# An attention network in one launch: in its first phase, buffers are taken in another order, more steps run side by side, and some work changes engine

## The chip, the cores and the metric

The program runs on one core of a Trainium2 chip. The metric is the device time of one execution in microseconds (us). A core has a matrix engine (TensorE, in the profile PE, its weight loads PEld), VectorE (DVE), ScalarE (ACT), GpSimd (POOL) and a queue engine (SyncE, SP) that issues transfers here. Each engine works through its own list of instructions in order and waits at semaphores for the others. Before the change the time is 3989.45 us, the median of three runs (3988.71 to 3994.0).

## What is computed

The input is a batch of 32 sequences of 256 tokens with 256 features, float32 throughout. Two layers follow each other. The change is in the first layer, up to its router; this is the kernel's first phase. Cut to what matters, for each sequence:

```python
k  = modulated(x, cond)                       # 256x256 matrix, scaled by the condition
# softmax over the 16 heads of each token: weights q_h . q_h', used on the same 16 heads
o0 = head_softmax_attention(k)
x0 = modulated(o0, cond)
# attention 1 over the 256 tokens, 16 heads of 16, on normed queries and keys
a  = softmax(norm(Q) @ norm(K).T / 4) @ V     # from x0
a  = a * sigmoid(g) * sigmoid(mean(gelu(x0 @ Wg1.T + bg1) @ Wg2.T + bg2))
x1 = x + a @ Wo.T + bo
c2 = x1 + relu(x1 @ w_down) @ w_up            # 256x64 and 64x256, scaled by the condition
h  = layer_norm(c2)
c2 = c2 + attention_2(h)                      # plain queries and keys
logits = layer_norm(c2) @ wr                  # for the router of the second phase
```

The second phase (from the router on: eight experts, the second layer, a butterfly network) uses some of the same helpers. It begins when all 32 sequences are through the first phase.

## The kernel before

**Staging.** One sequence is written as a Python generator, `sequence(b, exact)`. It issues its instructions in steps, and ahead of each it yields the engine and a length, for instance `yield PE, 1.75`. `side_by_side` is a planner: it holds all 32 generators and always lets that step go next which can start first by its own bookkeeping of engines and lengths. So the order of the instructions on each engine is fixed when the program is built; on the chip nothing is reordered. A step that calls another generator with `Part(...)` and yields it runs beside its caller from there on; `yield "join", part` waits for its end.

**Buffers.** `ring` makes a pool of n tiles with a queue of turns (`Turns(n)`), `get` waits for a turn and takes a tile, `back` returns it. `mm` has 3 PSUM tiles, `sh` 12 tiles of 128x512 in SBUF, `hp` 3 large ones, `kk` 2, `qk` 3, `kT` 3, `x1` 3, `c2` 3. `lanes = Turns(6)` lets six sequences be on the way at once.

**One sequence, step by step**, with the lines of the kernel before:

- xT is loaded (L830), scaled on ScalarE (L833), multiplied on TensorE (L252), moved out by ScalarE (L841), transposed back (L246), and copied twice side by side into `kk` by ScalarE (L851).
- `head_softmax_attention` (`exact` is False on the branch that runs): VectorE multiplies `kk` with itself shifted by j heads (L490) and sums over 16 features (L495), for j from 0 to 8; ScalarE takes the exponential (L518); `mirror` on GpSimd fills j from 9 to 15 from these by symmetry with 14 small copies (L503, L504); VectorE sums the weights (L523), inverts (L524), multiplies each weight with its window of `kk` (L531) and adds up in a tree (L539 to L543). The tile `hex` holds the weights as [token half, j, head].
- `transposed` transposes a tile on TensorE (L240) and moves it out on ScalarE (L289, L293). Here and in most steps the PSUM tile is taken from `mm` before the SBUF tile for the result.
- `gate_of_heads` (L764 to L784) runs to its end before attention 1 begins.
- `attention`: `cosine_queries_and_keys` does the two token halves one after the other: projection (L566), bias (L573), squares on ScalarE (L576), sums (L579); then a power on GpSimd (L208, L210) and the scaling (L559), which is a part of its own. Then scores (L716, four 32-row tiles of the array at once), exponentials on ScalarE (L725, 128x2048 at a time), answers (L698, four 32-column tiles at once), copies (L705), transposes back (L743), and a division (L749, L750), one token half after the other.
- `adapter_weights` makes the two small matrices on GpSimd (L795 to L800); they are used at L906 and L915, with ScalarE's ReLU at L910 between them and VectorE's addition at L919 after them.
- `layer_norm`: VectorE takes the statistics (L306, L307), GpSimd the inverse root (`rsqrt`, L208, L210), VectorE scales (`normalize`, L232).

Of the kernel before, what the change touches and what calls it, by code (L numbers as in the profile page):

```python
# [14 lines left out]
F = mybir.dt.float32  # L15
# [7 lines left out]
P = 128  # L23
# [143 lines left out]
def network(ctx: ExitStack, tc: tile.TileContext, a: dict, out: bass.AP):  # L167
# [113 lines left out]
    def transposed(x2, name, scale=None, bias=None, r="sh"):  # L281

        ps = yield from get("mm", "mm", TS)
        yield PE, 0.55
        transpose2(ps, x2)
        xT = yield from get(r, name, TS)
        if scale is None and bias is None:
            yield ACT, 0.6
            nc.scalar.copy(xT, ps)  # L289
        else:  # L290
            yield ACT, 0.95
            for c in range(2):
                nc.scalar.activation(  # L293
                    xT[:, c, :], ps[:, c, :], AF.Identity, bias=bias(c) if bias else 0.0, scale=scale(c) if scale else 1.0
                )
        yield back("mm")
        return xT

    def layer_norm(sm, x2, name):

        yield DVE, 1.2
        st = sm.tile([P, 2, 6], F, name="st")
        mv = sm.tile([P, 2, 2], F, name="mv")
        rstd = sm.tile([P, 2], F, name="rstd")
        for t in range(2):
            nc.vector.bn_stats(st[:, t, :], x2[:, t, :])  # L306
            nc.vector.bn_aggr(mv[:, t, :], st[:, t, :])  # L307
        yield POOL, 1.0
        rsqrt(rstd, mv[:, :, 1], 2, LN_EPS)
        xh = yield from get("sh", name)  # L310
        yield DVE, 0.75
        normalize(xh, x2, mv, rstd)
        return xh
# [118 lines left out]
    wdn = load_w(wA, "wdn", HID)  # L432
    wup = wA.tile([HID, D], F, name="wup")
    nc.sync.dma_start(wup, a["wup"])
    wr = load_w(wA, "wr", NE)
# [27 lines left out]
    ring(pa, "hp", 3, [P, 8, D])  # L463
    ring(pa, "sh", 12, [P, 2, D])
    ring(pa, "kk", 2, [P, 2, 2 * D])
# [15 lines left out]
    def head_softmax_attention(kk, o0, b, exact):  # L481


        e = sm.tile([P, 2, H, H], F, name="hex", tag="hex", bufs=3)
        for j0 in range(0, 9, 4):
            n = min(4, 9 - j0)
            r = "hp" if n == 4 else "sh"
            pr = yield from get(r, "hprod", [P, 2, n, D])
            yield DVE, 0.57 * n
            nc.vector.tensor_tensor(  # L490
                pr, kk[:, :, :D].unsqueeze(2).to_broadcast([P, 2, n, D]), windows(kk, j0, n), ALU.mult
            )
            for t in range(2):
                yield DVE, 0.3 * n
                nc.vector.tensor_reduce(  # L495
                    e[:, t, j0 : j0 + n, :], pr[:, t].rearrange("p j (h d) -> p j h d", d=DH), AX.X, ALU.add
                )
            yield back(r)
# [8 lines left out]
        if exact:  # L507
            yield POOL, 2.8
            mirror()
            mx = sm.tile([P, 2, H], F, name="hmx")  # L510
            yield DVE, 1.7
            nc.vector.tensor_reduce(mx, e.rearrange("p t j h -> p t h j"), AX.X, ALU.max)
            nc.vector.tensor_tensor(e, e, mx.unsqueeze(2).to_broadcast([P, 2, H, H]), ALU.subtract)
            yield ACT, 0.6
            nc.scalar.activation(e, e, AF.Exp, scale=scale)
        else:
            yield ACT, 0.45
            nc.scalar.activation(e[:, :, :9, :], e[:, :, :9, :], AF.Exp, scale=scale)  # L518
            yield POOL, 2.8
            mirror()  # L520
        rs = rhead[:, 2 * b : 2 * b + 2, :]
        yield DVE, 1.5
        nc.vector.tensor_reduce(rs, e.rearrange("p t j h -> p t h j"), AX.X, ALU.add)  # L523
        nc.vector.reciprocal(rs, rs)  # L524
        for t in range(2):
            prs = []
            for j0 in (0, 8):
# [4 lines left out]
                    pr.rearrange("p j (h d) -> p j h d", d=DH),  # L532
                    e[:, t, j0 : j0 + 8, :].unsqueeze(3).to_broadcast([P, 8, H, DH]),
                    windows(kk, j0, 8)[:, t].rearrange("p j (h d) -> p j h d", d=DH),
# [16 lines left out]
    def cosine_queries_and_keys(hT, qT, kT):  # L551
# [8 lines left out]

        halves = []
        for t in range(2):
            ps = yield from get("mm", "mm", [P, 2 * H, DH])
            yield PE, 1.75
            for c in range(2):
# [3 lines left out]
                )  # L569
            qk = yield from get("sh", "qk", [P, 2 * H, DH])  # L570
            sq = yield from get("sh", "sq", [P, 2 * H, DH])
            yield DVE, 0.7
# [7 lines left out]
            yield back("sh")  # L580
            p = Part(normed(qk, n2))
            yield p
            halves.append((p, qk))
        for p, _ in halves:
            yield "join", p
        for side in range(2):
            ps = yield from get("mm", "mm", TS)
# [83 lines left out]

    def attention(l, hT, o_n, b, exact):

# [8 lines left out]
        else:  # L682
            yield from plain_queries_and_keys(hT, qT, kT)
            yield vals
        yield "join", vals
        yield back("sh")
# [51 lines left out]
        yield "back", vaug_turn[l]  # L738
        for t in range(2):
            ps = yield from get("mm", "mm", [P, H, 32])  # L740
# [14 lines left out]
            )  # L755
            yield back("mm")
        yield back("avT")

    def gate_of_heads(x0T, gate, bgate):

        ps = yield from get("mm", "mm", TS)
        yield PE, 0.9
        for c in range(2):
            nc.tensor.matmul(ps[:, 0, :], wg1[:, c, :], x0T[:, c, :], start=(c == 0), stop=(c == 1))  # L764
        gj = yield from get("sh", "gj", [P, S])
        gs = sm.tile([P, 1], F, name="gs")
# [19 lines left out]
    def adapter_weights(b, wd, wu):  # L786
        g1 = yield from get("sh", "dgbb", [P, 2 * HID])
        g2 = yield from get("sh", "ugbb", [HID, 2 * D])
        yield SP, 0.1
        nc.sync.dma_start(g1, gtab[b : b + 1, : 2 * HID].to_broadcast([P, 2 * HID]))  # L790
        yield SP, 0.1
        nc.sync.dma_start(g2, gtab[b : b + 1, 2 * HID :].to_broadcast([HID, 2 * D]))
        yield None, 2.5
# [27 lines left out]

    lanes = Turns(6)

    def sequence(b, exact):
# [7 lines left out]
        for c in range(2):  # L832
            nc.scalar.mul(xT[:, c, :], xT[:, c, :], sty["k"][:, c, b : b + 1])  # L833
        ps = yield from get("mm", "mm", TS)
        yield PE, 1.75
        project_T(ps, wT["k"], xT)
        yield back("sh")
        kxT = yield from get("sh", "kxT", TS)
        yield ACT, 1.05
        for m in range(2):  # L840
            nc.scalar.activation(  # L841
                kxT[:, m, :], ps[:, m, :], AF.Identity, bias=col("kb", m), scale=dem["k"][:, m, b : b + 1]
            )
        yield back("mm")
        ps = yield from get("mm", "mm", [P, 2, D])
        yield PE, 0.55
        transpose2_back(ps, kxT)
        yield back("sh")
        kk = yield from get("kk", "kk")
        yield ACT, 1.05  # L850
# [7 lines left out]
        o0T = yield from transposed(o0, "o0T", scale=lambda c: sty["o"][:, c, b : b + 1])  # L858
        yield back("sh")
        ps = yield from get("mm", "mm", TS)  # L860
        yield PE, 1.75
        project_T(ps, wT["o"], o0T)
        yield back("sh")
        x0T = yield from get("sh", "x0T", TS)
        yield ACT, 1.05
# [8 lines left out]
        bgate = sm.tile([P, 2], F, name="bgate")  # L874
        yield from gate_of_heads(x0T, gate, bgate)
        o_n = yield from get("sh", "o_n")
        yield from attention(1, x0T, o_n, b, exact)
        x = yield from get("sh", "x")
        res = Part(residual_in(b, x))
        yield res  # L880
        wd = sm.tile([P, 2, HID], F, name="wd", bufs=2)
        wu = sm.tile([HID, D], F, name="wu", bufs=2)
        wts = Part(adapter_weights(b, wd, wu))
# [3 lines left out]
        )  # L887
        yield back("sh")
        ps = yield from get("mm", "mm", [P, 2, D])
        yield PE, 1.75  # L890
        project(ps, oT, wout[1])
        yield back("sh")
        yield "join", res
        x1 = yield from get("x1", "x1")
        yield DVE, 0.7
# [3 lines left out]


        x1T = yield from transposed(x1, "x1T")
        yield "join", wts
        ps = yield from get("mm", "mm", TS)
        yield PE, 0.9
        for c in range(2):
            nc.tensor.matmul(ps[:HID, 0, :], wd[:, c, :], x1T[:, c, :], start=(c == 0), stop=(c == 1))  # L906
        yield back("sh")
        act = yield from get("sh", "act", [HID, S])
        yield ACT, 0.5
        nc.scalar.activation(act, ps[:HID, 0, :], AF.Relu)  # L910
        yield back("mm")
        ps = yield from get("mm", "mm", [P, 2, D])
        yield PE, 0.9
        for t in range(2):
            nc.tensor.matmul(ps[:, t, :], act[:, t * P : (t + 1) * P], wu, start=True, stop=True)  # L915
        yield back("sh")
        c2 = yield from get("c2", "c2")
        yield DVE, 0.7
        nc.vector.tensor_add(c2, ps, x1)  # L919
        yield back("mm")  # L920


        xh = yield from layer_norm(sm, c2, "xh")
        hT = yield from transposed(xh, "hT", scale=lambda c: col("ln1g", c), bias=lambda c: col("ln1b", c))
# [18 lines left out]
        yield res  # L943
        xh = yield from layer_norm(sm, c2, "xh")
        yield "join", res
# [1207 lines left out]
```

## Time and profile before

| | us |
|---|---|
| median of three runs | 3989.45 |
| the profiled execution, whole | 3993.62 |
| its span, first to last instruction | 3991.9 |
| first instruction of the head products on VectorE (L490) | 37.67 |
| first scores of an attention on TensorE (L716) | 171.16 |
| last store of the first phase (L948) begins | 1826.43 |
| first instruction of the second phase on VectorE (L1059) | 1834.34 |

Busy in the whole span: PE 3627.3 us, DVE 2471.0 us, ACT 1787.2 us, POOL 1979.5 us.

How to read it: an engine's busy time is the union of its instructions. A group's row gives line, engine, operation, output and input tiles with their shapes and the count, then busy time and mean duration of one instruction, then the idle time of the engine just before these instructions with the one who ended it. Each float32 matmul leaves two records, so counts of PE rows are twice the program's. TensorE's granted clock (PEclk) is a share of full speed.

### The profile page before, as it was taken

How to read it: one execution, taken by the hardware profiler on the slowest of the kernel's cores; microseconds unless marked ns; L12 is line 12 of the kernel's file. 1: busy time of each engine (PE TensorE's matmuls, PEld its weight loads, DVE VectorE, ACT ScalarE, POOL GpSimd, SP SyncE). 2: the span in 40 equal slices, each digit the busy share in tenths (PEclk: the TensorE clock that was granted, in tenths of full speed). 3: DMA queues.
4: the chain of work that ended last, by engine and by line, in shares of the span. 5: the costliest groups of instructions: out<-in, count | busy, mean ns of one | idle time of the engine just before them, and what ended most of it. 6: DMA issues, size and time to landing. Idle time of an engine off the chain costs nothing. (4 is left out here: it accounts for less than half of the span.)

```text
span 3991.9 us, 55591 instructions
## 1 busy us (share of the span) xinstructions
PE 3627.3 (91%) x21868; PEld 2607.7 (65%) x21869; DVE 2471.0 (62%) x3951; ACT 1787.2 (45%) x2682; POOL 1979.5 (50%) x1959
## 2 busy tenths in 40 slices
PE   2689898899999999887999999999898999999999
PEld 2356556566666666552566666666686888888888
DVE  6886898898999999625766452000236464565654
ACT  1367666667777777662222222222222333333333
POOL 4554445545555555420644656554215455565653
PEclk7699999999999999995899999999998999999999
DMA  1001000000000000002233433322242323232331
GB/s 63 5 16 32 22 24 15 26 26 26 26 26 26 27 28 26 23 18 90 74 99 91 106 88 85 62 47 48 67 157 77 104 83 104 88 116 87 100 102 43
DMA packets 134368, 237.17 MB, mean 59 GB/s; under 512 B 19249, under 2 KB 80817, under 8 KB 131538
## 3 DMA queue, kind: packets, MB, share of 16 engines
q0 software_dynamic: 48128, 100.77, 10.4%
q1 hardware_dynamic: 85826, 132.25, 9.9%
q8 instruction: 174, 2.85, 0.3%
q14 instruction: 96, 0.79, 0.1%
q10 hardware_dynamic: 144, 0.52, 0.0%
HBM read 182.99 MB, written 50.48 MB: 58 GB/s over the span
## 5 line engine op out<-in xcount | busy, mean ns | idle before, releaser
L725 ACT ACTIVATE pt<-sc 128x2048 f32<-128x2048 f32 x256 | 480.7, 1878 | 204.1 <-PE sc L716 202.0
L1373 PE MATMUL by<-w,hid 128*128 128x256 f32 x2048 | 452.7, 379 | 2.5 <-DVE ysb L1379 2.5
L1358 PE MATMUL bh<-ehT,w 128*128 128x512 f32 x1024 | 452.3, 595 | 1.5 <-ACT ehT L1327 1.5
L1347 ACT ACTIVATE hid<-bh,cols 128x512 f32<-128x512 f32 x256 | 174.8, 688 | 593.1 <-PE bh L1358 548.2
L1373 PEld LDWEIGHTS by<-w,hid 128*128 128x128 f32 x2048 | 386.5, 190 | 66.3 <-issue 13.9
L210 POOL TENSOR_TENSOR n<-n,negh 128x32 f32<-128x32 f32 x64 | 374.1, 5846 | 5.3
L1281 POOL DMA_INDIRECT rrows<-ysb,row x128 | 223.3, 1745 | 260.5 <-DMA rrows<-ysb,row 139.6
L698 PE MATMUL av<-pt,vaug 128*32 128x256 f32 x4096 | 292.0, 405 | 58.7 <-ACT pt L725 56.5
L1358 PEld LDWEIGHTS bh<-ehT,w 128*128 128x128 f32 x1024 | 194.9, 191 | 222.1 <-issue 215.9
L1379 DVE TENSOR_TENSOR ysb<-by,b 128x512 f32<-128x512 f32 x64 | 44.0, 688 | 454.4 <-PE by L1373 333.3
L716 PE MATMUL sc<-qT,kT 32*128 32x256 f32 x4096 | 306.1, 414 | 19.9 <-ACT pt L725 18.7
L539 DVE TENSOR_TENSOR hprod<-hprod 128x1024 f32<-128x1024 f32 (+2 forms) x384 | 317.0, 825 | 7.1
L531 DVE TENSOR_TENSOR hprod<-hex,kk 128x2048 f32<-128x2048 f32 x128 | 298.5, 2332 | 0.0
L716 PEld LDWEIGHTS sc<-qT,kT 32*128 32x128 f32 x4096 | 192.4, 192 | 131.4 <-issue 66.2
L1314 POOL DMA_INDIRECT xg<-h2buf,tok x128 | 150.3, 1174 | 211.5 <-DVE tok L1173 90.3
L1983 PE MATMUL dh<-zT,w_eff 128*128 128x256 f32 x1024 | 238.8, 383 | 5.7 <-DVE zT L1960 5.7
L698 PEld LDWEIGHTS av<-pt,vaug 128*32 128x32 f32 x4096 | 110.6, 113 | 188.1 <-ACT pt L725 86.3
L1997 PE MATMUL do<-w_con,gT 128*128 128x256 f32 x1024 | 231.7, 380 | 0.0
L1983 PEld LDWEIGHTS dh<-zT,w_eff 128*128 128x128 f32 x1024 | 191.2, 192 | 30.7 <-DVE zT L1960 6.9
L1997 PEld LDWEIGHTS do<-w_con,gT 128*128 128x128 f32 x1024 | 193.4, 191 | 25.4
L503 POOL COPY hex<-hex 128x30 f32<-128x30 f32 (+6 forms) x224 | 53.2, 237 | 308.8 <-ACT hex L518 308.8
L208 POOL TENSOR_SCALAR rstd<-mv 128x2 f32<-128x2 f32 x160 | 44.0, 275 | 317.8 <-DVE mv L307 309.9
(612 smaller groups left out, 7585.6 us busy)
## 6 DMA issues: line engine op xcount, KB each, us to landing
w<-in_w SPq DMA_DIRECT2D x16, 1024.0 KB
x<-rrows SPq DMA_DIRECT2D x64, 256.0 KB
bfw<-in_upw SPq DMA_DIRECT2D x10, 1024.0 KB
bfw<-in_dnw SPq DMA_DIRECT2D x10, 1024.0 KB
xT<-in_xT SPq DMA_DIRECT2D x32, 256.0 KB
x<-in_x SPq DMA_DIRECT2D x32, 256.0 KB
h2buf<-xh SPq DMA_DIRECT2D x32, 256.0 KB
ytbuf<-yT SPq DMA_DIRECT2D x32, 256.0 KB
```

What stands on the lines that cost most here:

```text
L210: nc.gpsimd.tensor_tensor(o, o, negh[:p].to_broadcast([p, n]), ALU.pow)
L531: nc.vector.tensor_tensor(pr.rearrange("p j (h d) -> p j h d", d=DH), e[:, t, j0 : j0 + 8, :].unsqueeze(3).to_broadcast([P, 8, H, DH]), wi ...
L539: nc.vector.tensor_tensor(pr[:, :n], pr[:, :n], pr[:, n : 2 * n], ALU.add)
L698: nc.tensor.matmul(av[32 * i : 32 * i + 32, c % 2, :], va[:, kc, 4 * c + i, :], pt[:, i, kc, :], start=(kc == 0), stop=(kc == 1),)
L716: nc.tensor.matmul(sc[:, i, kc, :], kT[r, m, kc * P : (kc + 1) * P], qT[r, e, m, :], start=True, stop=nm is None,)
L725: nc.scalar.activation(pt, sc, AF.Exp, scale=1.0 / math.sqrt(DH))
L1281: nc.gpsimd.indirect_dma_start(rrows[:, :], bass.IndirectOffsetOnAxis(ap=row[:, j0 + t : j0 + t + 1], axis=0), y[:, t, :], None, compute_o ...
L1347: nc.scalar.activation(o, ps, AF.Relu, bias=bcol)
L1358: nc.tensor.matmul(ps, w["w1"][:, c, f * P : (f + 1) * P], hT[c], start=(c == 0), stop=(c == 1))
L1373: nc.tensor.matmul(ps[:, t, :], hid[f // 4][:, f % 4, (t0 + t) * P : (t0 + t + 1) * P], w["w2"][:, f, :], start=(f == 0), stop=(f == 7),)
L1983: nc.tensor.matmul(ps[:, g, :], w_eff[:, c, f * P : (f + 1) * P], zT[:, c, :], start=(c == 0), stop=(c == 1))
L1997: nc.tensor.matmul(ps[:, t, :], gT[:, f, t * P : (t + 1) * P], w_con[:, f, :], start=(f == 0), stop=(f == 7))
```

## The change

Five things change in the first phase.

1. **Order of taking tiles.** In `transposed`, `half`, `gate_of_heads` and `sequence` the SBUF tile for the result is taken before the PSUM tile. `sh` grows from 12 to 16 tiles, `lanes` from 6 to 7.
2. **More parts.** The two halves of the cosine queries and keys, the two halves of the division after attention, and `gate_of_heads` become parts that run beside each other.
3. **Weights along a diagonal.** `mirror` goes from the branch that runs. `hex` is laid out as 24 rows of 9: rows 8 to 23 hold the heads with their j from 0 to 8, and ScalarE copies rows 16 to 23 to rows 0 to 7. Weights of j from 9 to 15 are read along a diagonal (step 9 between heads, step 8 between j). The sum of the weights takes two reductions and an addition.
4. **Layer norms of the first phase** are scaled on ScalarE with scale and bias per token; GpSimd makes the bias with two more small operations. In the second phase `layer_norm` stays as it was.
5. **Adapter.** Both small products use the array in two 64-wide tiles, one for each token half. `wup` is loaded to both partition halves, and `wu` and `act` fill 128 partitions.

The diff, cut to its core:

```diff
     def transposed(x2, name, scale=None, bias=None, r="sh"):
+        xT = yield from get(r, name, TS)
         ps = yield from get("mm", "mm", TS)
         yield PE, 0.55
         transpose2(ps, x2)
-        xT = yield from get(r, name, TS)
...
-    def layer_norm(sm, x2, name):
+    def layer_norm(sm, x2, name, engine=DVE):
...
         rsqrt(rstd, mv[:, :, 1], 2, LN_EPS)
+        if engine == ACT:
+            less = sm.tile([P, 2], F, name="less")
+            nc.gpsimd.tensor_scalar(less, mv[:, :, 0], -1.0, None, ALU.mult)
+            nc.gpsimd.tensor_tensor(less, less, rstd, ALU.mult)
+            xh = yield from get("sh", name)
+            yield ACT, 0.95
+            for t in range(2):
+                nc.scalar.activation(
+                    xh[:, t, :], x2[:, t, :], AF.Identity, bias=less[:, t : t + 1], scale=rstd[:, t : t + 1]
+                )
+            return xh
...
-    ring(pa, "sh", 12, [P, 2, D])
+    ring(pa, "sh", 16, [P, 2, D])
...
-        e = sm.tile([P, 2, H, H], F, name="hex", tag="hex", bufs=3)
+        hex_ = sm.tile([P, 2, H * H], F, name="hex", tag="hex", bufs=3)
...
+            e = hex_[:, :, : 24 * 9].rearrange("p t (h j) -> p t h j", j=9)
+        def weights(t, j0, n, t1=None):
...
+            if j0 < 8:
+                return e[:, ts, 8:, j0 : j0 + n].rearrange("p t h j -> p t j h")
+            v = e[:, ts, 0:1, 0:1]
+            return bass.AP(v.tensor, v.offset + 9 * 0 + 8 + 8 * (j0 - 8), [v.ap[0], v.ap[1], (8, n), (9, H)])
...
-            nc.scalar.activation(e[:, :, :9, :], e[:, :, :9, :], AF.Exp, scale=scale)
-            yield POOL, 2.8
-            mirror()
+            nc.scalar.activation(e[:, :, 8:, :], e[:, :, 8:, :], AF.Exp, scale=scale)
+            nc.scalar.copy(e[:, :, :8, :], e[:, :, 16:, :])
...
-        nc.vector.tensor_reduce(rs, e.rearrange("p t j h -> p t h j"), AX.X, ALU.add)
+            nc.vector.tensor_reduce(rs, e[:, :, 8:, :], AX.X, ALU.add)
+            nc.vector.tensor_reduce(rs2, weights(0, 9, 7, 2).rearrange("p t j h -> p t h j"), AX.X, ALU.add)
+            nc.vector.tensor_add(rs, rs, rs2)
...
-                    e[:, t, j0 : j0 + 8, :].unsqueeze(3).to_broadcast([P, 8, H, DH]),
+                    weights(t, j0, 8)[:, 0].unsqueeze(3).to_broadcast([P, 8, H, DH]),
...
-        halves = []
-        for t in range(2):
+        def half(t, o):
+            qk = yield from get("sh", "qk", [P, 2 * H, DH])
+            sq = yield from get("sh", "sq", [P, 2 * H, DH])
             ps = yield from get("mm", "mm", [P, 2 * H, DH])
...
+        halves = []
+        for t in range(2):
+            o = []
+            p = Part(half(t, o))
             yield p
...
-        for t in range(2):
+        def tokens(t):
             ps = yield from get("mm", "mm", [P, H, 32])
...
-    lanes = Turns(6)
+    lanes = Turns(7)
+    pair_turn = Turns(1)
...
+        kk = yield from get("kk", "kk")
         ps = yield from get("mm", "mm", [P, 2, D])
         yield PE, 0.55
         transpose2_back(ps, kxT)
         yield back("sh")
-        kk = yield from get("kk", "kk")
...
-        yield from gate_of_heads(x0T, gate, bgate)
+        gates = Part(gate_of_heads(x0T, gate, bgate))
+        yield gates
         o_n = yield from get("sh", "o_n")
-        yield from attention(1, x0T, o_n, b, exact)
+        yield from attention(1, x0T, o_n, b, exact, gates)
...
         for c in range(2):
-            nc.tensor.matmul(ps[:HID, 0, :], wd[:, c, :], x1T[:, c, :], start=(c == 0), stop=(c == 1))
...
+            for t in range(2):
+                nc.tensor.matmul(
+                    ps[t * HID : (t + 1) * HID, 0, :P], wd[:, c, :], x1T[:, c, t * P : (t + 1) * P],
+                    start=(c == 0), stop=(c == 1),
+                )
...
+        c2 = yield from get("c2", "c2")
+        yield pair_turn
+        ps = []
         for t in range(2):
-            nc.tensor.matmul(ps[:, t, :], act[:, t * P : (t + 1) * P], wu, start=True, stop=True)
...
+            ps.append((yield from get("mm", "mm", [P, D])))
+        yield "back", pair_turn
+        yield PE, 0.6
+        for t in range(2):
+            r = slice(t * HID, (t + 1) * HID)
+            nc.tensor.matmul(ps[t], act[r, :], wu[r, :], start=True, stop=True)
...
+        for t in range(2):
+            nc.vector.tensor_add(c2[:, t, :], ps[t], x1[:, t, :])
...
-        xh = yield from layer_norm(sm, c2, "xh")
+        xh = yield from layer_norm(sm, c2, "xh", ACT)
```

The last edit stands twice. The names in the second phase that call the changed `transposed` are `side_part` and `whole`; the second phase's instructions stand in the same order on every engine before and after the change. In the first phase the program before has 7319 instructions on TensorE's list, 2105 on VectorE's, 1618 on ScalarE's and 958 on GpSimd's; the changed one has 7383, 2073, 1778 and 638.

## The prediction, made before the changed kernel ran

> **What bounds the kernel now.** The second phase has the same order of instructions on every engine before and after, so only the first phase counts: 1834.34 us of the span of 3991.9 us. I read the page's slices first, then busy times by stage, then who waited for whom, then the start in order of time, then the groups that the edits touch.
>
> The slices (each 99.8 us):
>
> ```profile
> PE   2689898899999999887999999999898999999999
> DVE  6886898898999999625766452000236464565654
> PEclk7699999999999999995899999999998999999999
> ```
>
> TensorE and VectorE are both nearly full from the third slice to the 17th; TensorE comes late at the start, VectorE ends early.
>
> Busy time by stage (us, instructions in brackets; then granted clock):
>
> ```profile
> 37.00:200.00 163.00, 69.17 (x301) 39.96 (x299) 146.15 (x164) 41.98 (x64) 69.26 (x85) 0.62 0.01 3
> 200.00:830.00 630.00, 561.26 (x4668) 369.24 (x4668) 521.04 (x737) 419.51 (x590) 302.82 (x339) 0.95 0.07 23
> 830.00:1697.00 867.00, 805.89 (x6971) 535.77 (x6969) 760.88 (x1115) 620.59 (x877) 478.85 (x488) 0.99 0.09 26
> 1697.00:1834.00 137.00, 109.38 (x950) 71.08 (x950) 30.08 (x76) 70.56 (x91) 27.59 (x32) 0.85 0.06 20
> ...
> sum 600.00, PE 564.63 PEld 376.57 DVE 543.80 ACT 439.51 POOL 338.16; mean PE 188.21 PEld 125.52 DVE 181.27 ACT 146.50 POOL 112.72
> ```
>
> The columns are PE, PEld, DVE, ACT, POOL. PE is busy 89.1% from 200 to 830 us, 93.0% from 830 to 1697, 79.8% in the tail. The last row covers 1000 to 1600 us by stretches of 200 us. There the loads of xT (L830) start at 1040.82 and, eleven sequences later, at 1585.13: 49.48 us a sequence. Times 188.21/200 that is 46.6 us of PE for each sequence; DVE has 44.8, ACT 36.2, POOL 27.9. So PE is the fullest, VectorE only 1.7 us behind, and some 2.9 us of a sequence's period is PE standing idle.
>
> Who waited, from 37 to 1834 us (total, times, longest):
>
> ```profile
> PE av L698 <- ACT pt L725: 56.5, 41, 2.6
> PE mm L246 <- ACT kk L851: 33.5, 1, 33.5
> PE mm L240 <- ACT kk L851: 31.1, 1, 31.1
> DVE rd L749 <- PE mm L743: 61.8, 13, 20.8
> DVE qk L559 <- POOL n L210: 57.0, 28, 5.3
> DVE rhead L523 <- POOL hex L504: 18.5, 14, 5.1
> ```
>
> The two single waits of over 30 us are the start:
>
> ```profile
> 78.76 0.43 DVE L543 TENSOR_TENSOR o<-o,rhead 128x256 f32<-128x256 f32 x1
> 108.17 1.01 ACT L851 COPY kk<-mm 128x1024 f32<-128x1024 f32 x1 [27.12 <-DVE hprod L531]
> 109.23 1.12 PE L240 MATMUL mm<-ident,o 128*128 128x128 f32 x4 [31.14 <-ACT kk L851]
> ```
>
> The first sequence's o0 is ready at 79.2 us, but its transposition runs at 109.23: ahead of it in PE's list stand transpositions of later sequences, which hold PSUM tiles while they wait for one of two `kk` tiles.
>
> The groups that the edits touch:
>
> ```profile
> L915 PE MATMUL mm<-wu,act 64*128 64x256 f32 x128 | 36.1, 402 | 0.0
> L906 PE MATMUL mm<-x1T,wd 128*64 128x256 f32 x128 | 34.5, 392 | 0.0
> L232 DVE TENSOR_SCALAR xh<-c,mv,rstd 128x256 f32<-128x256 f32 x128 | 48.0, 417 | 20.6 <-POOL rstd L210 20.6
> L523 DVE TENSOR_REDUCE rhead<-hex 128x32 f32<-128x512 f32 x32 | 32.8, 1026 | 18.5 <-POOL hex L504 18.5
> L531 DVE TENSOR_TENSOR hprod<-hex,kk 128x2048 f32<-128x2048 f32 x128 | 298.5, 2332 | 0.0
> ```
>
> **The change, part by part.** Costs are for all 32 sequences.
>
> Adapter: 34.5 + 36.1 = 70.6 us of PE. Two tiles of the array at once halve this: -35 us. That tiles run at once shows in L716, four 32-row tiles: 4096 records of 414 ns mean fill only 306.1 us, and L698 does the same with columns. The other bound: tiles one after the other, L915 unchanged and L906 as 256 records of 128 columns at the 0.16 us (81.6/512) that L743's records take, 41 us instead of 34.5: +6. I take -35, since L716 and L698 are the same kind. These instructions lie on the fullest engine; at 93% busy they are worth 35/0.93 = 38 us. Beside it: `wu` grows to 128 partitions with the same 256 columns, so L799 and L800 keep their times; `ugbb` is twice as many bytes and `wup` one more load on SP's queue, at a DMA share of 0.09 and with nobody waiting for these tiles: nothing. VectorE's addition becomes two of 256 columns, 0.42 us each by L750, for one of 0.68: 5 us of VectorE, beside PE. The pair holds two of three PSUM tiles, which may delay a neighbour; the tiles freed early elsewhere weigh against that, and I take nothing.
>
> Norms: VectorE loses 48.0 us. ScalarE gains 128 instructions of about 0.50 us (L833, the same shape from SBUF): 64 us, 2.0 a sequence, to 38 of 49: it stays below PE. GpSimd gains two small operations per norm, each between 0.36 us (L208 on rstd) and 0.97 (L210 on rstd); I take 0.36, as neither is a power: 46 us, and 0.7 us more before the scaling may start. Behind the waiting scaling on ScalarE stand exponentials (L725), for which PE's answers wait. Bounds: nothing, or all 64 norms late on PE by 0.7, 46 us. Before, PE waited for xh in 9 of 64 norms; nine times 0.7 is 6 us, which I take.
>
> Mirror: GpSimd loses 53.2 us (L503) and 43.6 (L504), VectorE the wait of 18.5 at L523; ScalarE gains a copy of 144 elements, at most L518's 0.44 us, 14 us in all, beside PE's work.
>
> Sum of the weights: L523 reads with a step of 16 words, 1026 ns for 512 elements; L579 reads 512 in a row in 677. New: 288 in a row (0.38), 224 with a step of 8 (0.45 at L523's rate), an addition (0.2): 1.03. Nothing changes; bounds -3 and +10 us. The writes of L495 with a step of 9 are 64 for 1024 reads: nothing.
>
> Diagonal read in L531: bounds are nothing and L523's excess, 0.68 ns, on each of 2048 elements: 1.4 us for each of 128, 179 us of VectorE. I take nothing: each weight is repeated over 16 features, and L531 and L559 read such repeats now without a penalty (2.28 us for 2048, 0.66 at best for 512), so a hop comes once in 16: 11 us at most. VectorE ends at 44.8 - 1.5 + 0.2 = 43.5 us a sequence, under PE's 46.6 - 1.1 = 45.5.
>
> [...]
>
> Order of tiles, parts, lanes: in the changed PE list the first o0 is transposed before the third sequence's kk, and the first scores come before the second sequence's projections; before, two sequences go in lockstep and the first scores run at 171.16. Worth between 0 and 45 us (30 of waiting, 15 of lockstep) of work started earlier; I take 25. It counts only while PE stays the bound to the end, as the sums say. Lanes and `sh` cost no instruction; a tile held longer costs nothing while 16 suffice.
>
> Packing: from 200 to 830 us PE is 89.1% busy; less the adapter's share, 561 - 12 = 549 us take 616 at that and 590 at the 93.0% of the next stage: -26. For it: I counted, by mean durations, the PE work that stands in PE's list between a product and the first matmul that reads its moved-out copy. Under 2.2 us (L725's 1.88 and a hand-over) stand in 304 of 1410 places before and 235 after. Against it: among scores to answers, the dearest wait, it is 58 of 256 before and 62 after. Past 93% I take nothing; at 95% the later stage would give 18 us more.
>
> **Sum**: -38 - 25 - 26 + 6 = -83 us. The profiled execution took 3993.62 us, 4 above the median, so 3910.6 there and 3907 as a median (3989.45 - 83).
>
> **The rivals.** Only the removed work is felt: in-order lists stall as before and no start is gained, -38 + 6 = -32, 3957. For it: the waits of L698, unchanged. Better than forecast: 45 at the start and 95%, -83 - 20 - 18 = -121, 3868. For it: fewer waits through GpSimd. No net effect: the norms' 46 us on ScalarE eat the 38 of the adapter and the order gives nothing: 3997. Slower: the diagonal costs its upper bound in L531. VectorE then needs 43.5 + 4 x 1.4 = 49.1 us a sequence and is the bound; at 94% busy, the best that PE has now, a period of 52.2, 2.7 more than 49.48; over 28 sequences +76, less 25 of the start: +51, 4040. VectorE overtakes PE when L531 passes 2.28 + 0.50 = 2.8 us; the gain is gone near 3.3 us. Against it: L559.
>
> **How the numbers follow.** Forecast 0.56 (own range 3880 to 3940), only work 0.19, better 0.11, no net effect 0.05, slower 0.09. A measurement of this kernel tells about 0.2%, 8 us, from no change. The first three are faster: 0.86; same 0.05; slower 0.09. The range 3855 to 3985 leaves out slower, most of no net effect, and about a third of better.
>
> **What would show it.** Right: the first phase ends near 1750 us, the adapter's two groups near 35 us together, L531's successor at 2.3 us, the waits of 30 us on kk gone, first scores near 125 us, PE at 93% or more from 200 us on, the second phase as long as before. Wrong: L531 at 3 us or more, ScalarE waiting long for GpSimd at the norms with PE behind it, or a tail above 137 us.

## The result, and the profile after

The changed kernel is slower: 4030.22 us, median of four runs (4024.9 to 4034.74), beside 3989.08 for the kernel before on the same chip; the ratio is 1.010, 95% interval 1.0082 to 1.0118. The profiled execution took 4034.14 us, with a span of 4032.4. The second phase begins at 1876.05 us instead of 1834.34; from there to the end of the span it is 2156.4 us, before 2157.6. All of the loss lies in the first phase.

The slices of the page after (PE, DVE, granted clock; each 100.8 us):

```profile
PE   3788999989888988886999999999898999999999
DVE  6889868797888777624766453000136564555654
PEclk7799999899999999997799999999998999999999
```

TensorE starts earlier (3 and 7 instead of 2 and 6), but from the 11th slice to the 18th it stands at 8 but for one, and VectorE is no longer full either. No engine has become the bound: from 830 to 1697 us each of them is busy for less of the time than before. The stages say it in numbers (PE, PEld, DVE, ACT, POOL, then clock):

```profile
37.00:200.00 163.00, 91.24 (x616) 57.72 (x618) 148.44 (x178) 67.65 (x99) 60.01 (x26) 0.74 0.03 8
200.00:830.00 630.00, 558.44 (x4660) 370.14 (x4660) 526.65 (x766) 437.44 (x647) 322.70 (x229) 0.94 0.08 25
830.00:1697.00 867.00, 761.16 (x6430) 506.83 (x6431) 699.67 (x1024) 606.57 (x887) 417.13 (x310) 0.94 0.08 26
```

The 22 us that TensorE gains up to 200 us are there. From 830 to 1697 us it is busy 87.8%, before 93.0%, and its clock is 0.94 instead of 0.99. The start itself, in the trace after:

```profile
79.15 0.90 PE L240 MATMUL mm<-ident,o 128*128 128x128 f32 x3 [14.32 <-DVE o L581]
109.91 2.09 PE L762 MATMUL sc<-qT,kT 32*128 32x256 f32 x16 [0.98 <-ACT kT L646]
```

The transposition of the first o0 runs 30 us earlier and the first scores 61 us earlier. So the start came earlier, as forecast, and was lost again later. Waits of the first phase (total, times, longest):

```profile
ACT xh L317 <- POOL less L313: 83.3, 35, 6.3
PE av L744 <- ACT pt L771: 72.3, 61, 3.9
DVE rhead L559 <- ACT hex L550: 45.2, 18, 5.6
```

The first row is new: at 35 of the 64 norms ScalarE stands, up to 6.3 us, for the product `less` that GpSimd now computes. The answers' wait for exponentials, 56.5 us before, is 72.3. The groups that the edits made:

```profile
L317 ACT ACTIVATE xh<-c,less,rstd 128x256 f32<-128x256 f32 x128 | 69.7, 593 | 83.4 <-POOL less L313 83.3
L979 PE MATMUL mm<-wu,act 64*128 64x256 f32 x128 | 28.1, 469 | 6.4 <-DVE c L1003 6.2 <-DVE qk L611 0.2
L962 PE MATMUL mm<-x1T,wd 128*64 128x128 f32 x256 | 22.4, 299 | 5.3 <-POOL wd L848 3.3 <-ACT x1T L289 2.0
L569 DVE TENSOR_TENSOR hprod<-hex,kk 128x2048 f32<-128x2048 f32 x128 | 297.7, 2325 | 0.0
```

The adapter takes 50.5 us of TensorE instead of 70.6; the diagonal read costs nothing (2325 ns, before 2332).

One norm in order of time shows what a wait of ScalarE does (start, length, engine, line; in brackets the idle time before it):

```profile
1133.54 1.26 POOL L864 TENSOR_TENSOR rs__9374<-x,c 128x512 f32<-128x512 f32 x1
1134.88 0.52 POOL L208 TENSOR_SCALAR rstd<-mv 128x2 f32<-128x2 f32 x1
1135.49 0.77 POOL L210 TENSOR_TENSOR rstd<-rstd,negh 128x2 f32<-128x2 f32 x1
1136.32 0.38 POOL L312 TENSOR_SCALAR less<-mv 128x2 f32<-128x2 f32 x1
1136.52 2.28 DVE L521 TENSOR_TENSOR hprod<-kk 128x2048 f32<-128x2048 f32 x1
1136.79 2.07 POOL L313 TENSOR_TENSOR less<-less,rstd 128x2 f32<-128x2 f32 x1
1138.90 1.09 ACT L317 ACTIVATE xh<-c,less,rstd 128x256 f32<-128x256 f32 x2 [4.79 <-POOL less L313]
1140.05 0.57 ACT L751 COPY avT<-av 128x512 f32<-128x512 f32 x1
1140.67 1.07 PE L744 MATMUL av<-pt,vaug 128*32 128x256 f32 x16 [2.38 <-ACT avT L751]
1141.67 1.89 ACT L771 ACTIVATE pt<-sc 128x2048 f32<-128x2048 f32 x1
```

GpSimd needs 4.0 us from the first of the norm's four operations to the end of the last. In the planner's bookkeeping the whole step has 1.0 (`yield POOL, 1.0` stands ahead of four operations where there were two). ScalarE has come to the norm's place in its list and stands 4.79 us. The copy L751 behind it belongs to another sequence; TensorE's answers wait 2.38 us for that copy, not for the norm. And the exponential L771, whose scores were there at 1138.3, starts 3.4 us later.

### The profile page after: what moved, and what is told of

Its sections match the earlier page's. It is cut to its first block, busy times and chain, and to the rows that moved or that the text cites. A ratio compares the mean times of both kernels' runs of the same rounds, so it can differ in the third digit from the quotient of the medians.

```text
span 4032.4 us, 55509 instructions
## 1 busy us (share of the span) xinstructions
PE 3637.3 (90%) x21997; PEld 2621.0 (65%) x21997; DVE 2424.4 (60%) x3919; ACT 1853.6 (46%) x2842; POOL 1942.9 (48%) x1639
## 5 line engine op out<-in xcount | busy, mean ns | idle before, releaser
L771 ACT ACTIVATE pt<-sc 128x2048 f32<-128x2048 f32 x256 | 481.1, 1879 | 167.6 <-PE sc L762 166.3
L744 PE MATMUL av<-pt,vaug 128*32 128x256 f32 x4096 | 296.4, 410 | 79.2 <-ACT pt L771 72.3
L577 DVE TENSOR_TENSOR hprod<-hprod 128x1024 f32<-128x1024 f32 (+2 forms) x384 | 314.8, 820 | 8.4
L569 DVE TENSOR_TENSOR hprod<-hex,kk 128x2048 f32<-128x2048 f32 x128 | 297.7, 2325 | 0.0
L208 POOL TENSOR_SCALAR n<-n 128x32 f32<-128x32 f32 x64 | 58.7, 917 | 484.0 <-DVE n L617 395.9
L208 POOL TENSOR_SCALAR rstd<-mv 128x2 f32<-128x2 f32 x160 | 52.6, 328 | 383.1 <-DVE mv L307 375.1
```

Source lines behind the costliest of these rows:

```text
L569: nc.vector.tensor_tensor(pr.rearrange("p j (h d) -> p j h d", d=DH), weights(t, j0, 8)[:, 0].unsqueeze(3).to_broadcast([P, 8, H, DH]), wi ...
L577: nc.vector.tensor_tensor(pr[:, :n], pr[:, :n], pr[:, n : 2 * n], ALU.add)
L744: nc.tensor.matmul(av[32 * i : 32 * i + 32, c % 2, :], va[:, kc, 4 * c + i, :], pt[:, i, kc, :], start=(kc == 0), stop=(kc == 1),)
L771: nc.scalar.activation(pt, sc, AF.Exp, scale=1.0 / math.sqrt(DH))
```

## The experiments

Theory L: the order was laid on a length for the norms' GpSimd step that is far too short. Theory N, its strict form: the way through GpSimd costs wherever it is put. Theory D: the exponential and copy of the heads' weights on ScalarE are the loss. Theory S: any new order lands somewhere else, and no edit is to blame. The table has the changed kernel and the 18 runs after it; "length" is what the planner counts for the norms' step on GpSimd, "hand-over" its time between engines, the wait is that of ScalarE for `less` in the first phase. The 1.7, 2.4 and 3.4 in the three rows below the changed kernel, and the 0.25 of "before, replanned", hold for the second phase too; in all other rows the number differs in the first phase alone. The ends and waits are those of one profiled execution each.

| kernel | norms, length | hand-over | median us | ratio to before, 95% | first phase ends | wait |
|---|---|---|---|---|---|---|
| changed | ScalarE, 1.0 | 0.2 | 4030.2 | 1.0082–1.0118 | 1876.1 | 83.3 |
| same, 1.7 | ScalarE, 1.7 | 0.2 | 4023.3 | 1.0061–1.0095 | 1853.8 | 67.6 |
| same, 2.4 | ScalarE, 2.4 | 0.2 | 3970.3 | 0.9936–0.9969 | 1808.2 | 47.8 |
| same, 3.4 | ScalarE, 3.4 | 0.2 | 3970.4 | 0.9928–0.9962 | 1804.9 | 27.3 |
| norms on VectorE | VectorE | 0.2 | 3957.5 | 0.9899–0.9935 | 1797.5 | – |
| changed, replanned | ScalarE, 1.0 | 0.25 | 4012.8 | 1.0042–1.0075 | 1857.0 | 110.2 |
| same, 2.4 | ScalarE, 2.4 | 0.25 | 3965.0 | 0.9926–0.9959 | 1812.7 | 40.5 |
| norms on VectorE | VectorE | 0.25 | 3924.9 | 0.9819–0.9852 | 1768.8 | – |
| before, norms alone | ScalarE, 1.0 | 0.2 | 4074.9 | 1.0187–1.0221 | 1923.4 | 97.0 |
| before, replanned | VectorE | 0.25 | 4014.9 | 1.0037–1.0082 | 1872.6 | – |
| before, replanned | VectorE | 0.15 | 4065.4 | 1.0169–1.0203 | 1911.5 | – |
| before, diagonal alone | VectorE | 0.2 | 4000.2 | 1.0019–1.0040 | 1841.2 | – |
| before, adapter alone | VectorE | 0.2 | 3982.2 | 0.9980–1.0000 | 1826.6 | – |
| order alone | VectorE | 0.2 | 3983.7 | 0.9989–1.0008 | 1828.4 | – |
| changed, mirror on GpSimd | ScalarE, 1.0 | 0.2 | 4054.2 | 1.0135–1.0169 | 1887.7 | 136.5 |
| changed, six lanes | ScalarE, 1.0 | 0.2 | 4046.5 | 1.0118–1.0152 | 1892.5 | 112.7 |
| norms on VectorE, all lengths | VectorE | 0.2 | 3941.5 | 0.9873–0.9906 | 1792.8 | – |
| changed, all lengths | ScalarE, 2.4 | 0.2 | 3957.7 | 0.9920–0.9954 | 1801.6 | 62.5 |
| norms on VectorE, all lengths | VectorE | 0.25 | 3972.1 | 0.9956–0.9977 | 1819.5 | – |

**Norms back on VectorE.**

```diff
-        xh = yield from layer_norm(sm, c2, "xh", ACT)     # both norms
+        xh = yield from layer_norm(sm, c2, "xh")
```

> The changed kernel with one part undone: both norms are scaled by VectorE again, as before the change; all else stays. Theory N (the norms are the loss: ScalarE stands 83 us behind GpSimd's product L313, and the exponentials behind it make TensorE late): about 40 us or more come back, 3990 us or less, and TensorE is above 92% busy between 1000 and 1600 us again. Theory D (the loss is VectorE waiting in order for ScalarE's exponential and copy of the heads' weights): the time stays near 4030 us, since ScalarE loses only 70 us of work. Theory S (each new plan of the order lands somewhere within about 1%, whatever the edit): any time between 3960 and 4060, and nothing to read from it alone.

Measured 3957.5: 73 us come back, nearly twice what the change loses. From 1000 to 1600 us TensorE is busy 91.2%, in the changed kernel 87.4%. D in its plain form falls, since ScalarE's part in the heads' weights is still there.

**Only the number in the planner.**

```diff
-        yield POOL, 1.0
+        yield POOL, 2.4        # then 1.7 and 3.4
         rsqrt(rstd, mv[:, :, 1], 2, LN_EPS)
```

> The changed kernel, in which the planner of the order counts 2.4 us for the norms' four operations on GpSimd instead of 1.0; the trace shows 0.50 + 0.97 + 0.54 + 0.43 us for them. No instruction is changed, only their order. Theory L (the loss comes from the order, which puts ScalarE's scaling where GpSimd cannot have it ready): the waits of 83 us for the product fall below 40, and 20 to 40 us come back, 3990 to 4010. Theory N in its strict form (the way through GpSimd is too long wherever it is placed): 4020 to 4040. Theory S: between 3960 and 4060, with no link between the waits and the time.

> The changed kernel with 1.7 us in the planner for the norms' four operations on GpSimd, between the 1.0 that gave 4030 and the 2.4 that gave 3970. Theory L: between them, 3985 to 4015, and the wait of ScalarE for the product between 48 and 83 us. Theory S: anywhere between 3950 and 4050.

> The same with 3.4 us, one more than the mean of the trace, since single operations there took up to 2.3 us. Theory L: the wait falls further, below 40 us, and the time stays within 10 us of 3970 or goes toward the 3957 of norms on VectorE: 3955 to 3980. Theory S: anywhere between 3950 and 4050.

No instruction differs, and 60 of the 73 us come back at 2.4; L had expected 20 to 40 and a wait below 40 us. Waits in the trace at 2.4:

```profile
ACT xh L317 <- POOL less L313: 47.8, 25, 7.3
PE av L744 <- ACT pt L771: 71.8, 54, 3.5
```

From 1.0 to 3.4 the wait goes 83, 68, 48, 27 us, and the first phase ends at 1876, 1854, 1808, 1805. The whole time at 1.7 is 4023, above L's 3985 to 4015: `layer_norm` serves the second phase too, whose part of the span was 2170 us there and 2166 at 3.4, 2157 at 2.4.

TensorE's wait for the exponentials does not move with the number (72.3 us at 1.0, 71.8 at 2.4; with the norms on VectorE it is 71.6), so the time does not come back there. Among its waits that fall from 1.0 to 2.4 are those for `xh`, from 23.5 to 7.1 us, and for `x1`, the sum before the adapter (L950), from 42 to 14. The number also tells the planner when GpSimd is free again, so it moves other steps than the norms. Through which waits the 60 us come back is not separated.

**The norms alone, on the kernel before.** The edit is `layer_norm` of the change, and nothing else.

> The kernel before with one part of the change alone: both norms scaled by ScalarE, GpSimd's step still counted as 1.0 by the planner of the order. Theory N/L (this part is the loss, because the order expects the product 1.4 us too early): slower than before, by the 30 to 70 us that undoing it gave back, 4020 to 4060, with ScalarE waiting 60 to 120 us for the product. My forecast's own view (6 us): 3995 or less. Theory S (any new order lands within about 1%): 3950 to 4030, no link with that wait.

Measured 4074.9, 83 more and above the 4060 of N and L, with a wait of 97 us. The forecast's 6 us fall.

**Is it luck of an order?** One number of the planner, in the kernel before.

```diff
-LAG = 0.2
+LAG = 0.25      # and, for the first phase alone, 0.15
```

> The kernel before, in which only one number of the planner differs: the hand-over between engines is counted as 0.25 us instead of 0.2. Not one instruction changes, only their order. This measures how far a new order alone moves the time. Theory S: 20 to 40 us either way. Theory L: within 10 us of 3989, since no length in the plan has become wrong.

> The kernel before with the hand-over counted as 0.15 us instead of 0.2 in the planner of the first phase alone; no instruction changes. The other direction of a new order (0.25 ended the first phase 38 us later). Theory S, symmetric: anywhere within 40 us of 3989. If the order of before stands better than its neighbours: later again, 4000 to 4030. Theory L: within 10 us of 3989.

Measured 23 and 76 us slower; L's 10 us were missed both times. S has a point: in the second run a new order alone costs nearly as much as the whole change was to win. With 0.25 the second phase was planned anew too and is 21 us shorter; by the first phase alone the two orders end 38 and 77 us later. Both neighbours are worse, so the order of before stands better than these two. A single comparison of two plans settles nothing below some 80 us, and the norms had to be tried again under a second plan.

**The same pair under a second plan.** The hand-over is 0.25 in the first phase alone, in all three.

> The changed kernel with the hand-over counted as 0.25 us in the planner of the first phase alone; the norms' step stays at 1.0. If the loss comes from the norms' length (N, L) and not from an unlucky order: still slower than before, 4000 to 4060, with 60 us or more of ScalarE waiting for the product. If it was an unlucky order (S): likely below 3990.

> The changed kernel with the norms on VectorE and the hand-over counted as 0.25 us in the first phase alone. N and L: still faster than before, 3935 to 3980, so that the distance to the replanned changed kernel of the same call is 40 to 110 us again. S: the distance shrinks below 30 us or changes its sign.

> The changed kernel with its norms on ScalarE, the hand-over counted as 0.25 us in the first phase, and the norms' four operations on GpSimd counted as 2.4 us instead of 1.0. Under the first plan that one number gave 60 us. Theory L (the order was laid on a length that is too short): 3940 to 3975, 40 to 70 less than the 4012.8 of the same plan at 1.0, and the wait of ScalarE for the product falls from 110 us below 70. Theory N, strict (the way through GpSimd costs wherever it is put, and the first pair was luck): within 20 us of 4013. Theory S: anywhere between 3930 and 4040.

Norms on ScalarE and VectorE: 4012.8 and 3924.9, 88 apart; the second is faster than the 3935 expected at best. With the length at 2.4: 3965.0, 46 less by the ratios. The loss of the norms is thus there under two plans and in the kernel before (73, 88, 83), and the number alone gives 60 and 46 of it. Most of these differences are below 80 us; what speaks for L is that they agree. Whatever else differs in them, the six kernels with the norms on ScalarE and a length of 1.0 or 1.7 take 4012.8 to 4074.9, the four with 2.4 or 3.4 take 3957.7 to 3970.4. ScalarE's wait does not give the time by itself: it is 110.2 us at 4012.8 and 83.3 at 4030.2, 62.5 at 3957.7 and 47.8 at 3970.3. What remains to the norms on VectorE is 13 and some 42 us; how much of that is N and how much another order is open. Fewer GpSimd operations for the product were not tried.

Whether the five parts together lose is another question, and its answer depends on the plan. With 0.25 on both sides the changed kernel's first phase ends 16 us before that of the kernel before (1857.0, 1872.6), with 0.2 it ends 42 us after it.

**The other parts.** The mirror on GpSimd again, in the changed kernel; six lanes; and three parts by themselves: the diagonal read on the kernel before, the adapter on the kernel before, and the order (tiles, parts side by side, seven lanes, 16 tiles) without the other three.

```diff
-    lanes = Turns(7)
+    lanes = Turns(6)
```

> The changed kernel with one part undone: the heads' weights are mirrored by GpSimd again (L503 and L504 of the kernel before) and read in order, one sum over 16. Theory D: VectorE's wait of 45 us for ScalarE at rhead turns back into one of about 18 for GpSimd, the period falls from 56 toward 50 us, about 4000 us. Theory N: GpSimd gets 97 us more work, so its product for the norms comes later still: 4030 to 4070. Theory S: between 3960 and 4060.

> The changed kernel with six sequences in flight instead of seven (the 16 tiles stay). Theory lanes (the seventh sequence adds tiles held and work that stands ahead of older sequences): about 3990. Theories N and D: no more than 10 us either way, 4020 to 4040, since the start is the same and only 49.5 us a sequence is lost later. Theory S: between 3960 and 4060, although not one instruction of the work is changed.

> The kernel before with the diagonal read of the heads' weights alone (no mirror on GpSimd, exponential and copy on ScalarE, two sums on VectorE). The forecast took nothing for this part, 3989. Undoing it in the changed kernel made that 24 us slower, so theory G (GpSimd's 97 us of mirroring stood before the power step and the norms, whose results VectorE and ScalarE wait for) expects 3955 to 3975 and the waits of VectorE at L559 for the power step (57 us before) cut by a third or more. Theory S: within 25 us of 3989 either way, no link with those waits.

> The changed kernel without the adapter's two tiles, without the diagonal read and with the norms on VectorE: what is left is the order of tiles, the parts side by side, seven lanes and 16 tiles. The forecast gave this part 25 us at the start and 26 in the packing: 3938 by it. If only the start is gained (the first scores come 60 us earlier in the trace of the changed kernel, and TensorE does 20 us more by 200 us): 3964 to 3970. If the gain is given back later, TensorE at 89% from 200 to 830 us as before: 3985 or more. A new order alone moved the kernel before by 23 us, so less than that is not told apart.

> The kernel before with the adapter's two tiles of the array alone (and its three PSUM tiles of which the pair takes two). The forecast halved 70.6 us of TensorE and divided by 0.93: 38 less, 3951. By the durations in the trace of the changed kernel (L962 22.4 and L979 28.1 us, 50.5 together) it is 20.1/0.93 = 22 less, 3967. If the pair's PSUM tiles hold up their neighbours: 3980 or more. A new order alone moved the kernel before by 23 us.

The mirror costs 24 us in the changed kernel, 12 of them in the first phase, and its removal 11 us in the kernel before: the sign changes with the plan, so nothing can be said on G's time, and the 24 us may be the order as well. G's sign did come: without the mirror VectorE's wait at the scaling of q and k for the power step falls from 57.0 to 34.7 us. The 4000 us that D expected with the mirror back did not come. Six lanes are slower by 16, so nothing speaks for the seventh as the loss. The adapter alone gives 0.1%; the order alone nothing. Where the start goes is in the stages of the order alone:

```profile
37.00:200.00 163.00, 86.32 (x567) 53.82 (x565) 148.16 (x168) 63.59 (x91) 71.94 (x81) 0.72 0.02 6
830.00:1697.00 867.00, 790.39 (x6657) 527.18 (x6655) 743.97 (x1061) 596.65 (x835) 437.13 (x458) 0.96 0.08 25
```

TensorE does 17 us more by 200 us, and 15.5 us less from 830 to 1697 (790.4, before 805.9).

**All lengths as measured.** Projections 1.95 for 1.75, the power step 6.6 for 5.8, scaling of q and k 1.0 for 0.7, the router 1.1 for 0.4, and so on.

> The changed kernel with the norms on VectorE, and every length in the planner of the first phase set near the mean that the trace of the changed kernel shows (projections 1.95 for 1.75, power step 6.6 for 5.8, router 1.1 for 0.4, adapter 0.7 and 0.9 for 0.6 and 0.6, and so on). Theory L in its wide form (the loss is a plan with wrong lengths, whichever they are): better than the 3957 of norms on VectorE, 3920 to 3950. In its narrow form (only lengths on a chain that makes an engine wait in order matter, and the norms' was the one): within 25 us of 3957. Theory S: 3930 to 4000.

> The changed kernel with its norms on ScalarE, with all lengths of the first phase set as measured, the norms' step on GpSimd at 2.4 us among them. Theory L, wide: below the 3970 of the norms' length alone, 3910 to 3950, since VectorE is 48 us freer than with the norms on it. Narrow: 3945 to 3995. Theory S: 3930 to 4010.

> The changed kernel with the norms on VectorE, all lengths of the first phase as measured and the hand-over at 0.25 us: both steps that were faster, 3941.5 and 3924.9, together. If measured lengths are worth something by themselves: 3900 to 3920. Theory S: between 3915 and 3965, with nothing added up.

3941.5 and 3957.7, by the ratios 11 and 6 us below the kernels without them, but some 50 us worse under the second plan (3972.1, there 3924.9 without them): nothing adds up, and L in its wide form is not borne out. Of the lengths tried, only that of the norms moved the time the same way under both plans. The fastest version is the changed kernel with norms on VectorE and a hand-over of 0.25: 3924.9, ratio 0.9835, 95% interval 0.9819 to 0.9852.

## Why the prediction was wrong, step by step

**Norms: the step that failed.** "Before, PE waited for xh in 9 of 64 norms; nine times 0.7 is 6 us, which I take." It measured +73 to +88. What it counted came near, before and then after:

```profile
PE mm L240 <- DVE xh L232: 14.5, 9, 3.8
PE mm L240 <- ACT xh L317: 23.5, 18, 4.5
```

That is 9 us more; the rest is what the step left out. Three things are wrong in it. It counted only who waits for xh; in the norm shown above, what stands behind the scaling on ScalarE pays too, another sequence's copy and an exponential. The text named such work, and then took nothing for it; what it costs over all 64 norms is not measured. It took 0.36 us for each new GpSimd operation; they take 0.54 and 0.43, and the whole step 2.36 (0.50 + 0.90 + 0.54 + 0.43) after 1.33 before. And it took the order of the changed list as laid out for these lengths: the new step stood under the old `yield POOL, 1.0`. By the runs this is the largest of the three, since that number alone gives 60 and 46 us back. The upper bound of 46 us left it out too, since it counted each norm once on PE.

**Adapter.** The prediction halved 70.6 us of PE and divided by 0.93: 38. In the adapter alone the two groups fall to 47.0 us (24.2 + 22.8), 50.5 in the changed kernel; so the halving is two thirds true. TensorE's busy time in the first phase falls by 20.3 us (1545.7 to 1525.4), its idle time rises by 12.6, and 7.7 us of the first phase are left. The division by 0.93 assumed that idle time shrinks with the work; it grew. How much of that is the adapter and how much the new order is open.

**Start and packing.** The events came (o0 at 79 us, scores at 110), the worth did not. "It counts only while PE stays the bound to the end, as the sums say" is the mistake: sums of busy time say who has most work, not that this engine never waits in its list. Packing took the 93.0% of the regular stage as a property of the work. It changes with the order: 90.2% in the kernel before at a hand-over of 0.25 (781.7 of 867 us), 91.2% in the order alone, 87.8% after.

**The base of the sum.** −83 was counted from an order that is 23 and 76 us better than its replanned neighbours. With the norms on VectorE the rest of the change gave −33 and −64 under two plans, both counted from the order of before, where the terms without the norms summed to −89. At the same hand-over on both sides, the first phase of these kernels ends 37 and 104 us before that of the kernel before (1797.5 and 1834.3, 1768.8 and 1872.6). How much of that each small term gave can't be told apart from what a new plan does.

**What was right.** L531's successor at 2.3 us, TensorE's waits of over 30 us for `kk` gone, the second phase as long as before, the rhead sum (0.45 + 0.55 + 0.20 = 1.20 us) near its 1.03. GpSimd's two operations on `wu` with 128 partitions for 64 take 0.72 us each at the shortest, as before, and 1.06 and 1.05 on the mean, before 0.87 and 1.66. Of the rivals, "no net effect" had the part that loses, the norms' way through GpSimd, at about half its size and without the planner's length; "slower" had the time, 4040, by luck, with a mechanism that L569 refutes (2325 ns, before 2332). The sign named for being wrong, ScalarE waiting long for GpSimd at the norms, is what the trace shows, with PE waiting directly behind it 18 times.

## What to carry to other kernels

In a schedule that is written down when the program is built, a length that is too short on the way to an in-order engine can cost the instructions queued there, not just the one that waits (in the norm shown, 2.38 us for another sequence's answers; the number alone gave 60 and 46 us back under two plans): after moving a step to another engine, correct its length from the trace first. Before giving a cause to one or two per cent, plan the same kernel anew with a neutral number: here that alone moved it by 0.6 and 1.9%, so each cause needs a second plan. Removed work on a 93% busy engine is not time won until its idle time is seen to stay: in the adapter alone 20.3 us less work came with 12.6 us more idle time, and 7.7 us were won.

## What the runs showed of the hardware

**At a mean clock of 0.92 TensorE was idle and busy for longer than at 0.94.** Changed kernel and norms on VectorE have the same TensorE instructions in the first phase (13018 records, another order). The windows of the first phase, changed and then norms on VectorE:

```profile
37.00:1876.05 1839.05, 1555.77 (x13018) 1029.97 (x13016) 1410.63 (x2059) 1218.83 (x1779) 842.94 (x622) 0.92 0.08 24
```

```profile
37.00:1797.48 1760.48, 1511.26 (x13018) 1008.69 (x13016) 1474.21 (x2187) 1162.83 (x1651) 786.62 (x492) 0.94 0.08 25
```

Of 78.6 us between them 34 are idle time and 44.5 are longer busy time, with a mean granted clock of 0.92 and 0.94; the 512 records of the projection L252 of `hT`, for one, take 416 and 402 ns on the mean. Fourteen of the kernels have these TensorE instructions in the first phase. At a mean clock of 0.92 (five kernels) TensorE is busy 1546 to 1556 us and idle 268 to 304, at 0.93 (five) 1524 to 1544 and 238 to 264, at 0.94 (four) 1505 to 1517 and 227 to 249. The other six have the TensorE instructions of the kernel before (12882 to 12894 records): at 0.92 (two) TensorE is busy 1583 to 1588 us and idle 286 to 304, at 0.93 (two) 1546 to 1548 and 243 to 252, at 0.94 (two) 1537 to 1551 and 267 to 285. Both times the kernels at 0.92 are busy and idle for longer than those at 0.94, among the six by 1 us of idle time in the nearest two; 0.93 does not always lie between them. That the idle time is what lowers the clock is not shown. The prediction had counted waits at their length only.

**A small GpSimd operation lasted up to 2.26 us while a large one of VectorE ran.** The two new operations on 128x2 elements (minimum, median and maximum in ns):

```profile
L312 POOL TENSOR_SCALAR less<-mv x64: 219/242/2258, 159.1 to 1866.7; 128x2 f32<-128x2 f32 x64
L313 POOL TENSOR_TENSOR less<-less,rstd x64: 194/196/2158, 161.4 to 1867.0; 128x2 f32<-128x2 f32 x64
```

Their medians are 0.24 and 0.20 us, their means 0.54 and 0.43. In the norm shown above L313 took 2.07 us and ended 0.06 us after VectorE's L521, 2.28 us long, a product with both operands from `kk` in SBUF. Of the 128 operations 31 took over 0.6 us, and each of the 31 ended 0.05 to 0.10 us after a VectorE operation with two operands in SBUF: a product (L521 five times, L569 seven) or an addition of the tree (L577, 19 times). 24 of the short ones ran wholly beside VectorE's sums over `hprod` (L526), which have one operand. Why the two end together is not shown.
